# Scaling on ScalarE and a single VectorE rounding in layer 2's quantized attention, and another order of routing for the first batch of its product-key layer

## The chip, the cores and the metric

The kernel runs on one core of a Trainium2 chip. A core has five engines that work side by side, each through its own queue of instructions in order: TensorE (PE in the profile; PEld is its weight load), VectorE (DVE), ScalarE (ACT), GpSimd (POOL) and SyncE (SP). They meet at semaphores, and DMA queues move data beside them. The metric is the device time of one execution in microseconds (us), lower is better. The kernel before has a median of 2180.47 us over three runs (2170.9 to 2184.78).

## The reference

A decoder of four layers, L0 to L3, over 8 sequences of 256 tokens with 256 features (2048 tokens). Each layer has attention, cross attention to a context and a feed-forward part, and after each of the twelve the input is added and the sum is normalised (`_layernorm`). Two neighbours matter here. Layer 2's cross attention is made of linear layers with quantized activations and ternary weights:

```python
def bitnet_linear(x, W, b):
    w_scale = jnp.maximum(jnp.mean(jnp.abs(W)), 1e-05)
    qW = jnp.sign(W) * (jnp.abs(W) > 0.5 * w_scale).astype(W.dtype)
    i_scale = jnp.maximum(jnp.max(jnp.abs(x)), 1e-08) / 127.0
    qx = jnp.clip(jnp.round(x / i_scale), -128.0, 127.0)
    return jnp.einsum('...i,oi->...o', qx, qW) * (w_scale * i_scale) + b
...
vis = bitnet_linear(dinov2_features, W_d2v, b_d2v)
image_embeds = bitnet_linear(vis, W_img, b_img)
fused = bitnet_linear(text_embeddings, W_txt, b_txt)
for Wa, ba in ((W_att0, b_att0), (W_att1, b_att1)):
    kv = bitnet_linear(image_embeds, Wa, ba)
    k = jnp.concatenate([kv, kv], axis=-1)
    attn = softmax(einsum('bse,bpe->bsp', fused, k) * inv_sqrt_e)
    fused = fused + 0.1 * einsum('bsp,bpe->bse', attn, k)
concatenated = [fused, broadcast mean of image_embeds]
h = jax.nn.relu(bitnet_linear(concatenated, W_f1, b_f1))    # 1024 wide
return bitnet_linear(h, W_f2, b_f2)
```

The step `i_scale` is taken from the largest absolute value of a whole activation, so a linear layer can begin only when the whole of its input is known.

Layer 2's feed-forward part looks up experts by product keys and adds a gated MLP:

```python
q = (hidden_states @ Wq.T), two halves of 4 heads
sim = jnp.einsum('pbthn,hkpn->pbthk', q, keys)         # 128 keys each half
sx, ix = top_k(sim[0], 8);  sy, iy = top_k(sim[1], 8)
all_scores = sx[..., :, None] + sy[..., None, :]       # 64 pairs
scores, pk = top_k(all_scores, 8)                      # 8 of 4096 experts a head
w = silu(einsum('btd,bthkd->bthk', x, down_embed[indices])) * softmax(scores)
experts_states = einsum('bthk,bthkd->btd', w, up_embed[indices])
mlp = silu(x @ Wg.T) * (x @ Wu.T) @ Wd.T
return mlp + experts_states
```

## The kernel before

The tokens lie in `self.X` as 16 tiles of 128 tokens (token on the partition) and, transposed, in `self.xT` (feature on the partition, 2 chunks of 128 x 2048). The source is written as generators, `woven` together (each is given with a number of steps and a share, and its steps are spread evenly over that share of the whole); within a stretch a scheduler then orders the instructions of each engine, so that the order on an engine is neither that of the source nor that of another engine. Tiles come from pools with a number of buffers each (`bufs`); an instruction that writes a tile waits until a buffer is free.

**The quantized attention** (`l2_xattn`, L2342). `quantize` (L2232) rounds one chunk with two VectorE instructions: L2236 multiplies by 1/step and adds ROUND, a constant that pushes the fraction out of float32; L2237 subtracts ROUND, takes the minimum with 127 and writes bfloat16. It is used in these places:

- the chunks of context and images, long before (in `prepare_l2_xattn`);
- X: `quantized` and `quantized_steps` (L2279) find the largest value (`all_max`), the step, its reciprocal `x_inv` (`step_of`), and round 8 chunks of 128x512 of `self.xT`; `bit_linear_T` then makes `fused` with TensorE and one VectorE instruction for each of its 8 chunks (L2337);
- the concatenation: after the two attention rounds (`bit_attend`), 8 chunks of `fused`, then the 16 columns of the average `avg` (into `qa`), from which 8 small matmuls and VectorE instructions (L2385) make `bias`, the part of the first linear layer that is the same for every token of a sequence, with its own bias;
- the hidden layer, which is computed twice. The first time (`hidden`, L2398) only the largest value of every row is taken: 4 blocks of 512 tokens x 8 rows of 128 hidden units, one VectorE reduction of 128x512 each into `top`. From it the step of the hidden layer follows. The second time each `hidden` goes through ScalarE as two Relu activations of 128x256 (L2416, scale `s1`, one bias column for a sequence) into `h`, is rounded into `qh` and multiplied by the second weight, eight matmuls into `po` for each of the block's four tiles; VectorE scales `po` and adds the residual (`z`, L2433; GpSimd has made the sum of X and the bias before, L2426), and `finish` normalises two tiles at a time: statistics (L178, L179) and the result X (L202) on VectorE, the reciprocal root on GpSimd (L156, L158), the transposition into xT on TensorE (L188) and ScalarE (L189).

**The product-key layer** (`l2_ffn`, `expert_batches`). It goes by batches of 256 tokens, two tiles each. `route` is a generator: the queries `qT` (L1824), then for each of the two tiles `product_keys` (L1617 on), which takes the 8 best of 128 for each head and half (L1629 copies the similarities on ScalarE; L1632 and L1633 search on VectorE), the 8 best of 64 pairs (L1646, L1647), the row numbers and the softmax (L1660 to L1678), and `compact_picks`, which packs the picks into 14 slots a token and lends the 15th to a token with too many (L1696 to L1746; L1723 writes `index`, L1735 is ScalarE's copy of what TensorE fetched for the lent slots, L1742 reads it). `gated` computes the eight chunks of the gate and up projections and their product `hT` (L1316 Silu on ScalarE, L1317 the product on VectorE).

The picks of a tile are fetched in four groups (4, 4, 4 and 3 rows a token) by GpSimd (`rows`, L1078, an indirect DMA for each of 15 picks) into four row buffers `rows0` to `rows3`, one for each group, used again by the next tile. VectorE takes the dot products with the token (`junk`, L1841), ScalarE their Silu, and TensorE adds the weighted second halves of the rows into `po` by diagonal matrices (L1923; the last row of a group of four goes through VectorE, L1914). `po` also takes the MLP (L1893), and at the end of a tile VectorE adds `rest` (L1931).

Routing of batch b+1 is woven into the picks of batch b (`later`, with the attention of layer 3 and its convolution). Only batch 0 has nothing ahead of it: its own routing, of both tiles, is woven with the gate (`own` beside `gate`) and is finished before its first pick is fetched in the source order.

Of the kernel before, what the change touches and what calls it, by code (L numbers as in the profile page):

```python
# [11 lines left out]
F32 = mybir.dt.float32  # L12
BF16 = mybir.dt.bfloat16
# [3 lines left out]
ALU = mybir.AluOpType  # L17
# [29 lines left out]
class Net:  # L47
# [1741 lines left out]
    def expert_batches(self, w, room, pool, work, ps, general):  # L1789
# [53 lines left out]
        def batch(b, conv, att):  # L1843
# [5 lines left out]
            here, state["routed"] = state["routed"], []  # L1849
            after = route(o + CH, state["routed"]) if b + 1 < B else iter(())  # L1850
# [21 lines left out]
            if b == 0:  # L1872
                for _ in woven((gate, 8, 1.0), (own, 20, 1.0)):
                    pass
            later = woven((gate, 8, 0.42), (after, 20, 0.8), (att, 17, 1.0), (conv, 12, 1.0))
            z = work.tile([P, 2, D], F32, name="z", bufs=1)
            for j in range(2):
                i = 2 * b + j
                x = self.X[:, i, :]
                index, prob, last, slot = here[j]  # L1880
# [357 lines left out]

    def ternary(self, pool):
# [39 lines left out]
    def quantized_steps(self, q, src, name, into, work, *weights, largest=None, bank=None):  # L2279
        n = src.shape[2]  # L2280
        m = self.all_max(src.rearrange("p c n -> p (c n)") if largest is None else largest, into, name, bank)
        inv, scales = self.step_of(m, [q[x][1] for x in weights], into, name)
        dst = into.tile([P, 2, n], BF16, name="q_act")
        for o in range(0, n, 512):
            for c in range(2):
                e = min(o + 512, n)
                self.quantize(dst[:, c, o:e], src[:, c, o:e], inv, work)
                yield
        return dst, scales
# [52 lines left out]
    def l2_xattn(self, w):  # L2342
        nc, tc = self.nc, self.tc
        FC = 8
        with (
# [7 lines left out]
            if True:  # L2353
                with tc.tile_pool(name="x2a", bufs=3, space=PSUM) as ps:
                    qx, (s,) = self.quantized(q, self.xT, "x", pool, work, "txt", largest=self.x_max)
                    self.bit_linear_T(fused, q["txt"][0], qx, s, self.col("l2x_b_txt"), ps)
                with tc.tile_pool(name="x2b", bufs=2, space=PSUM) as ps:
                    for n in range(2):
                        for b in range(B):
                            self.bit_attend(  # L2360
                                fused, kvT[:, n, b * SC : (b + 1) * SC], self.l2x_kv[:, n * B + b, :], b, work, ps
                            )
                            if n:
                                nc.vector.tensor_reduce(
                                    largest[:, b : b + 1], fused[:, :, b * S : (b + 1) * S], AX.XY, ALU.max,
                                    apply_absolute_value=True,
                                )
            m = self.all_max(largest, pool, "cat")
            inv, (s1,) = self.step_of(m, [q["f1"][1]], pool, "cat")
            qf = pool.tile([P, 2, NTOK], BF16, name="q_act")  # L2370
            for o in range(0, NTOK, 512):
                for c in range(2):
                    self.quantize(qf[:, c, o : o + 512], fused[:, c, o : o + 512], inv, work)
            qa = pool.tile([P, 2, B], BF16, name="qa")
            self.quantize(qa.rearrange("p c b -> p (c b)"), avg.rearrange("p c b -> p (c b)"), inv, work)
            w1, (w2, w2_scale) = q["f1"][0], q["f2"]
            with (
# [26 lines left out]
                inv, (s2,) = self.step_of(m, [w2_scale], pool, "hid")  # L2404
                b2 = late.tile([P, D], F32, name="b2")
# [3 lines left out]
                for o in range(0, NTOK, 512):  # L2409
                    qh = work.tile([P, FC, 512], BF16, name="qh")  # L2410
                    for f in range(FC):
                        pp = hidden(f, o)
                        h = work.tile([P, 512], F32, name="h")
                        for b in range(2):
# [6 lines left out]
                                scale=s1,  # L2421
                            )
                        self.quantize(qh[:, f, :], h, inv, work)
# [276 lines left out]
```

## Time and profile before

| what | value |
|---|---|
| median of three runs | 2180.47 us (2170.9 to 2184.78) |
| the profiled execution | 2177.3 us, its span 2175.4 us |
| mean granted TensorE clock | 0.933 of full speed |
| rounding of X, from its step to the end of `fused` | 1254.57 to 1266.59 us |
| the two attention rounds | 1266.65 to 1307 us |
| rounding of the concatenation, until the last row maximum | 1308.06 to 1337.29 us |
| hidden layer, second time | 1338.8 to about 1399 us |
| product-key layer, batch 0: from `qT` to the point where the orders of both kernels meet | 1403.25 to 1533.1 us |

A span is the time from the first to the last recorded instruction. The page gives, for the whole span, the busy time of each engine and the chain of work that ended last; other views give the busy time within a stretch, all instructions of a line or tile with their durations, and the instructions of an engine in order of time. In a timeline a row is: start, duration (of all instructions of the row together), engine, line, operation, output and inputs with shapes, how many, and in brackets how long the engine stood idle before it and what ended that. An average over the whole span says little about one stage: what a change there is worth is read from that stage's rows. Durations come from one execution.

### The profile page before, as it was taken

The numbers are of one execution on the slowest core, as the hardware profiler recorded it, in microseconds if no ns is written. First come the engines' busy times: TensorE is split into PE (matmuls) and PEld (weight loads), VectorE is DVE, ScalarE is ACT, GpSimd is POOL, SyncE is SP. The second block draws the span as 40 slices with busy tenths as digits, with TensorE's granted clock in tenths as the row PEclk, the third lists the DMA queues.
The fourth block names the chain that finished last, engine by engine and source line by source line (L and its number), as shares of the span: only waits on it lengthen the run. The fifth ranks groups of instructions, "written<-read, shape, count | busy, mean of one in ns | idle before, by whom it ended". The sixth has DMA issues, their size and how long they took to land. (4 is left out here: it accounts for less than half of the span.)

```text
span 2175.4 us, 37678 instructions
## 1 busy us (share of the span) xinstructions
PE 1890.9 (87%) x13612; PEld 1399.8 (64%) x13612; DVE 1566.4 (72%) x5213; ACT 891.1 (41%) x1982; POOL 680.8 (31%) x740
## 2 busy tenths in 40 slices
PE   7988699999998988997888877768899999998886
PEld 5765488755556666775555553456777777776775
DVE  5776445356666877765677678789999999976575
ACT  1332343333343334222434332434455554656663
POOL 1012245311111111644443101246444444431232
PEclk9999699999998988998999988888999999999998
DMA  4000355300002101884110010223323233220000
GB/s 138 2 2 13 121 182 172 125 2 1 1 2 92 43 29 46 245 242 121 40 40 21 8 66 10 77 79 93 85 78 86 65 86 90 79 90 15 6 15 21
DMA packets 71684, 148.49 MB, mean 68 GB/s; under 512 B 17000, under 2 KB 40056, under 8 KB 68416
## 3 DMA queue, kind: packets, MB, share of 16 engines
q0 software_dynamic: 32640, 79.46, 12.7%
q1 hardware_dynamic: 34218, 59.35, 8.3%
q10 hardware_dynamic: 4630, 7.16, 0.9%
q8 instruction: 111, 1.82, 0.3%
q14 instruction: 85, 0.70, 0.1%
HBM read 170.35 MB, written 23.24 MB: 89 GB/s over the span
## 5 line engine op out<-in xcount | busy, mean ns | idle before, releaser
L1078 POOL DMA_INDIRECT rows<-in_l2f_table_dram,index x240 | 252.8, 1053 | 280.5 <-PE po L1923 60.4
L146 PE MATMUL pp<-xT,w 128*128 128x256 f32 (+1 forms) x672 | 177.3, 406 | 11.7 <-ACT sim L1629 4.1
L668 POOL TENSOR_TENSOR aT<-sides,inv 128x256 f32<-128x256 f32 x64 | 47.1, 739 | 382.1 <-DVE sides L666 295.1
L146 PEld LDWEIGHTS pp<-xT,w 128*128 128x128 f32 x672 | 127.7, 197 | 37.3 <-ACT qT L1824 5.4
L189 ACT COPY xT<-pt 128x512 f32<-128x512 f32 x88 | 51.3, 585 | 184.1 <-PE pt L188 184.0
L188 PE MATMUL pt<-ident,X 128*128 128x128 f32 x352 | 70.1, 312 | 60.2 <-DVE X L202 44.0
L632 ACT ACTIVATE e<-sc 128x512 f32<-128x512 f32 (+1 forms) x145 | 77.5, 604 | 106.0 <-PE sc L560 82.1
L1923 PE MATMUL po<-rows,diag 128*128 128x256 f32 x384 | 108.7, 403 | 12.7 <-ACT diag L1922 12.2
L560 PE MATMUL sc<-kv,qv 32*128 32x128 f32 (+2 forms) x1540 | 111.5, 335 | 8.7 <-DVE sides L666 3.4
L560 PE MATMUL sc<-qv,kv 32*128 32x128 f32 (+2 forms) x1348 | 109.1, 353 | 3.2 <-DVE qv L614 1.7
L560 PEld LDWEIGHTS sc<-kv,qv 32*128 32x128 f32 x1540 | 88.4, 208 | 35.7 <-issue 20.7
L1078 POOL DMA_INDIRECT xe<-xd,take x83 | 82.4, 992 | 78.4 <-PE pt L1096 33.9
L156 POOL TENSOR_SCALAR rs_v<-ln_mv 128x2 f32<-128x2 f32 (+1 forms) x67 | 19.0, 284 | 279.6 <-DVE ln_mv L179 230.1
L188 PEld LDWEIGHTS pt<-ident,X 128*128 128x128 f32 x352 | 45.1, 154 | 91.3 <-DVE X L202 37.0
L146 PE MATMUL sc<-xT,w 128*128 128x512 f32 (+1 forms) x224 | 100.0, 594 | 2.2 <-DMA w<-in_l0a_wq_dram 1.5
L202 DVE TENSOR_SCALAR X<-z,ln_mv,rs_y 128x256 f32<-128x256 f32 x144 | 55.2, 425 | 59.2 <-POOL rs_y L158 59.1
L1236 ACT ACTIVATE hT<-ph,we_in 128x128 f32<-128x128 f32 x152 | 55.7, 367 | 95.1 <-PE ph L146 90.2
L1841 DVE SCALAR_TENSOR_TENSOR junk<-rows,X 128x256 f32<-128x256 f32 x224 | 93.5, 418 | 1.2
L560 PEld LDWEIGHTS sc<-qv,kv 32*128 32x128 f32 (+1 forms) x1348 | 75.1, 196 | 28.8 <-issue 17.1
L146 PE MATMUL ph<-xeT,we_in 128*128 128x128 f32 x608 | 87.7, 288 | 3.9 <-DMA we_in<-in_l0f_in_dram,wrow 2.5
L146 PEld LDWEIGHTS ph<-xeT,we_in 128*128 128x128 f32 x608 | 76.9, 194 | 15.8 <-ACT hT L1236 11.9
L1923 PEld LDWEIGHTS po<-rows,diag 128*128 128x128 f32 x384 | 68.1, 194 | 28.4 <-ACT diag L1922 16.9
(608 smaller groups left out, 5163.8 us busy)
## 6 DMA issues: line engine op xcount, KB each, us to landing
we<-in_l1f_experts_dram SPq DMA_DIRECT2D x32, 384.0 KB, 4.3
yd<-y SPq DMA_DIRECT2D x32, 256.0 KB
w<-in_l2x_w_dram SPq DMA_DIRECT2D x1, 4096.0 KB
v<-v SPq DMA_DIRECT2D x16, 243.8 KB, 2.7
rows<-in_l2f_table_dram,index POOLq DMA_INDIRECT x240, 3.3
xd<-X SPq DMA_DIRECT2D x8, 257.0 KB, 2.5
xT<-in_xT_dram SPq DMA_DIRECT2D x4, 512.0 KB, 9.2
X<-in_x_dram ACTq DMA_DIRECT2D x8, 256.0 KB
```

The source lines that it names most:

```text
L146: done = self.nc.tensor.matmul(out, lhsT=lhsT, rhs=rhs, start=n == 0, stop=n == last and bias is None)
L156: nc.gpsimd.tensor_scalar(v, var, LN_EPS, None, ALU.add)
L188: nc.tensor.transpose(pt[:, c, j, :], self.X[:, i0 + j * step, c * P : (c + 1) * P], self.ident)
L189: nc.scalar.copy(self.xT4[:, :, i0 : i0 + step + 1 : step, :], pt)
L202: nc.vector.tensor_scalar(self.X[:, i, :], z[:, j, :], mv[:, j, 0:1], r[:, j : j + 1], ALU.subtract, ALU.mult)
L560: nc.tensor.matmul(sc[: shape[0], part], lhsT=lhsT, rhs=rhs, start=mask is None, stop=True, skip_group_check=True)
L632: lambda r, sc: nc.scalar.activation(e0[m][:n0, r], sc, AF.Exp),
L668: nc.gpsimd.tensor_tensor(out, split(both), split(inv), ALU.mult)
L1078: return self.nc.gpsimd.indirect_dma_start(out=out, out_offset=None, in_=table, in_offset=bass.IndirectOffsetOnAxis(ap=index, axis=0), **( ...
L1236: nc.scalar.activation(hT[:, g + f, :], ph[:, f, :], AF.Gelu, bias=b1[:, g + f : g + f + 1])
L1841: nc.vector.scalar_tensor_tensor(junk, row, 1.0, x, ALU.mult, ALU.mult, accum_out=out)
L1923: nc.tensor.matmul(po, lhsT=diag, rhs=rows[:, k, D:], start=j == 0 and (g, k) == (0, 0), stop=j == 1 and (g, k) == (groups[-1][0], here_k ...
```

## The change

In the quantized attention, three of the uses of `quantize` are replaced. For X and for the concatenation ScalarE multiplies a chunk by 1/step (Copy with a scale column, three buffers), and VectorE rounds with one instruction, `rounded`, which adds and subtracts ROUND. In the hidden layer Relu's scale and bias are multiplied by 1/step beforehand (two small VectorE instructions), so that `h` is in steps already and VectorE only rounds it; `h` has three buffers in place of two. The minimum with 127 is dropped. The average's 16 columns are rounded ahead of the 8 chunks of `fused`. In the product-key layer batch 0's routing is woven with the gate only until the first tile's picks exist (`first_tile`); the rest of it, the second tile, stands in front of the other work in `later`, so that it is advanced between the first tile's picks, and what is left of it is finished before the second tile.

In the order of instructions that the build gives, the rest is the same: GpSimd issues the gathers in the same order, and from the second group of batch 1's first tile on all engines have the order of before.

```diff
--- before.py
+++ after.py
@@ -1847,6 +1847,12 @@
                 state["routed"] = []
                 own = route(0, state["routed"])
             here, state["routed"] = state["routed"], []
+
+            def first_tile():
+                while not here:
+                    next(own)
+                    yield
+
             after = route(o + CH, state["routed"]) if b + 1 < B else iter(())
             hT = work.tile([P, FC, CH], F32, name="hT", bufs=1)
 
@@ -1870,13 +1876,16 @@
 
             gate = gated()
             if b == 0:
-                for _ in woven((gate, 8, 1.0), (own, 20, 1.0)):
+                for _ in woven((gate, 8, 1.0), (first_tile(), 10, 1.0)):
                     pass
-            later = woven((gate, 8, 0.42), (after, 20, 0.8), (att, 17, 1.0), (conv, 12, 1.0))
+            later = chain(own, woven((gate, 8, 0.42), (after, 20, 0.8), (att, 17, 1.0), (conv, 12, 1.0)))
             z = work.tile([P, 2, D], F32, name="z", bufs=1)
             for j in range(2):
                 i = 2 * b + j
                 x = self.X[:, i, :]
+                if j == 1:
+                    for _ in own:
+                        pass
                 index, prob, last, slot = here[j]
                 at_end = work.tile([P, 1], F32, name="at_end")
                 dot(at_end, final[:, :D], x)
@@ -2236,6 +2245,14 @@
         nc.vector.tensor_scalar(t, src, inv, ROUND, ALU.mult, ALU.add)
         nc.vector.tensor_scalar(dst, t, ROUND, 127.0, ALU.subtract, ALU.min)
 
+    def rounded(self, dst, src):
+        self.nc.vector.tensor_scalar(dst, src, ROUND, ROUND, ALU.add, ALU.subtract)
+
+    def quantize_scaled(self, dst, src, inv, work):
+        t = work.tile([P, src.shape[-1]], F32, name="quant", bufs=3)
+        self.nc.scalar.activation(t, src, AF.Copy, scale=inv)
+        self.rounded(dst, t)
+
     def ternary(self, pool):
 
         nc = self.nc
@@ -2276,7 +2293,7 @@
             except StopIteration as stop:
                 return stop.value
 
-    def quantized_steps(self, q, src, name, into, work, *weights, largest=None, bank=None):
+    def quantized_steps(self, q, src, name, into, work, *weights, largest=None, bank=None, scaled=False):
         n = src.shape[2]
         m = self.all_max(src.rearrange("p c n -> p (c n)") if largest is None else largest, into, name, bank)
         inv, scales = self.step_of(m, [q[x][1] for x in weights], into, name)
@@ -2284,7 +2301,7 @@
         for o in range(0, n, 512):
             for c in range(2):
                 e = min(o + 512, n)
-                self.quantize(dst[:, c, o:e], src[:, c, o:e], inv, work)
+                (self.quantize_scaled if scaled else self.quantize)(dst[:, c, o:e], src[:, c, o:e], inv, work)
                 yield
         return dst, scales
 
@@ -2352,7 +2369,7 @@
             nc.vector.tensor_reduce(largest[:, B:], avg, AX.XY, ALU.max, apply_absolute_value=True)
             if True:
                 with tc.tile_pool(name="x2a", bufs=3, space=PSUM) as ps:
-                    qx, (s,) = self.quantized(q, self.xT, "x", pool, work, "txt", largest=self.x_max)
+                    qx, (s,) = self.quantized(q, self.xT, "x", pool, work, "txt", largest=self.x_max, scaled=True)
                     self.bit_linear_T(fused, q["txt"][0], qx, s, self.col("l2x_b_txt"), ps)
                 with tc.tile_pool(name="x2b", bufs=2, space=PSUM) as ps:
                     for n in range(2):
@@ -2367,12 +2384,14 @@
                                 )
             m = self.all_max(largest, pool, "cat")
             inv, (s1,) = self.step_of(m, [q["f1"][1]], pool, "cat")
+            qa = pool.tile([P, 2, B], BF16, name="qa")
+            qa_t = pool.tile([P, 2 * B], F32, name="qa_t")
+            nc.vector.tensor_scalar(qa_t, avg.rearrange("p c b -> p (c b)"), inv, None, ALU.mult)
+            self.rounded(qa.rearrange("p c b -> p (c b)"), qa_t)
             qf = pool.tile([P, 2, NTOK], BF16, name="q_act")
             for o in range(0, NTOK, 512):
                 for c in range(2):
-                    self.quantize(qf[:, c, o : o + 512], fused[:, c, o : o + 512], inv, work)
-            qa = pool.tile([P, 2, B], BF16, name="qa")
-            self.quantize(qa.rearrange("p c b -> p (c b)"), avg.rearrange("p c b -> p (c b)"), inv, work)
+                    self.quantize_scaled(qf[:, c, o : o + 512], fused[:, c, o : o + 512], inv, work)
             w1, (w2, w2_scale) = q["f1"][0], q["f2"]
             with (
                 tc.tile_pool(name="x2c", bufs=3, space=PSUM) as ps,
@@ -2402,6 +2421,9 @@
                 nc.vector.tensor_scalar(top, top, 0.0, None, ALU.max)
                 m = self.all_max(top.rearrange("p f b -> p (f b)"), pool, "hid")
                 inv, (s2,) = self.step_of(m, [w2_scale], pool, "hid")
+                in_steps = late.tile([P, 1], F32, name="in_steps")
+                nc.vector.tensor_tensor(in_steps, s1, inv, ALU.mult)
+                nc.vector.tensor_scalar(bias, bias, inv, None, ALU.mult)
                 b2 = late.tile([P, D], F32, name="b2")
                 pp = ps.tile([P, 512], F32, name="pp")
                 nc.tensor.matmul(pp[:, :D], lhsT=self.ones, rhs=b2_row, start=True, stop=True)
@@ -2410,7 +2432,7 @@
                     qh = work.tile([P, FC, 512], BF16, name="qh")
                     for f in range(FC):
                         pp = hidden(f, o)
-                        h = work.tile([P, 512], F32, name="h")
+                        h = work.tile([P, 512], F32, name="h", bufs=3)
                         for b in range(2):
                             n = o // S + b
                             nc.scalar.activation(
@@ -2418,9 +2440,9 @@
                                 pp[:, b * S : (b + 1) * S],
                                 AF.Relu,
                                 bias=bias[:, f, n : n + 1],
-                                scale=s1,
+                                scale=in_steps,
                             )
-                        self.quantize(qh[:, f, :], h, inv, work)
+                        self.rounded(qh[:, f, :], h)
                     for i in range(o // P, o // P + 4, 2):
                         z = work.tile([P, 2, D], F32, name="z")
                         nc.gpsimd.tensor_tensor(
```

## The prediction

> **What bounds the kernel now.** I read the page first (busy shares, then the chain of waits), then the busy time of each engine in the stretches that the diff touches, then the rows of the tiles and the timelines there. Busy shares, and the chain's shares by engine:
>
> ```profile
> PE 1890.9 (87%) x13612; PEld 1399.8 (64%) x13612; DVE 1566.4 (72%) x5213; ACT 891.1 (41%) x1982; POOL 680.8 (31%) x740
> PE 15%; DVE 12%; ACT 2%; POOL 1%; issue 1%; DMA 0%; POOLq 0%; ACTq 0%
> ```
>
> TensorE is the busiest over the span, but the averages hide the edited stages. Busy time by stretch (start:end, length, then each engine's busy us with instructions; then granted TensorE clock, DMA share, GB/s):
>
> ```profile
> 1254.00:1260.00 6.00, 3.05 (x8) 1.19 (x9) 5.59 (x18) 0.00 (x0) 0.00 (x0) 0.60 0.89 373
> 1307.00:1314.00 7.00, 0.58 (x2) 0.50 (x2) 6.29 (x20) 0.00 (x0) 0.00 (x0) 0.50 0.00 0
> 1338.00:1394.00 56.00, 42.17 (x214) 23.27 (x213) 47.76 (x122) 33.37 (x69) 15.14 (x20) 0.85 0.08 29
> 1403.20:1533.10 129.90, 98.94 (x443) 78.90 (x442) 110.73 (x550) 52.68 (x126) 64.09 (x61) 0.87 0.31 87
> 1520.00:1600.00 80.00, 71.51 (x364) 59.62 (x363) 76.23 (x365) 39.64 (x102) 39.18 (x38) 0.96 0.30 81
> ```
>
> The two rounding stretches (first two lines) are VectorE alone: ScalarE stands still and TensorE waits for rounded chunks. The hidden pass (1338 to 1394) has VectorE busy 47.76 of 56, the routing (1403.2 to 1533.1) 110.73 of 129.90, so 19.17 idle; after it VectorE is 95% busy. What is won on VectorE in these places is therefore won for the kernel, as nothing later has slack to absorb it.
>
> **X rounding.** The rows of the tile give 0.478 us for `quant<-xT` and 0.42 for `q_act<-quant`; the timeline has two of the first in 0.88 and two of the second in 0.75, so 0.73 a chunk, 8 chunks from 1254.76 to 1260.62, and then the 8 `fused` (L2337, 5.97 us) end at 1266.6. After: ScalarE scales 128x512 with a scale column. It did not do this form here; nearest is `qv<-turned,consts` (L1026), 0.714 us and two in 1.33, so a pitch of 0.62. The other bounds are the plain 128x512 copy of 0.585 (L189), pitch about 0.5, and `kv` of L1026 at 0.807. Eight copies from 1254.65 end at 1259.7 (7 × 0.62 + 0.71). The build puts VectorE's order as three rounds, one `fused`, two rounds, one `fused`, three rounds, six `fused`. The third round ends at 1257.05, `fused` 1 at 1257.8, rounds 4 and 5 at 1258.6, `fused` 2 at 1259.35, rounds 6 to 8 at 1260.5, six `fused` × 0.746 at 1265.0 to 1265.2. Gain **1.4** (0.4 at 0.8 a copy; 2.3 at 0.5).
>
> The Trainium skill ("ScalarE: Activation LUTs", Rules for kernel authors) says that a multiplication belongs on VectorE and not ScalarE, which speaks against this edit. The rows agree on speed (0.62 against 0.44 a chunk) but not on the advice, since ScalarE shows 0.00 busy here. By that rule alone the gain would be below zero by 8 × 0.18 = 1.4; by the rows it is 1.4.
>
> **Concatenation rounding.** Before: eight chunks from 1308.18 to 1314.1, the average's two operations, eight bias operations (1.64 us) from 1314.79, first row maximum (`top`, L2398) at 1317.14, the 32nd done at 1337.29. After: the average's 16 columns go first, so the bias work (TensorE and VectorE) lies under ScalarE's copies, which run from 1308.15 to 1313.2 by the same pitch. The build's order has seven rounds ahead of the first `top`; the seventh copy ends at 1312.6 and its round at 1313.0, so `top` starts near 1313.1 and one round (0.4) lies among the maxima. The 32 at the old pace (20.15) end at 1333.6. Gain **3.7** (bounds 2.5 and 4.5: copies at 0.8, or at 0.5).
>
> **Hidden pass.** What the rounding costs now, name and count first, then min/median/max ns:
>
> ```profile
> L2236 DVE TENSOR_SCALAR quant<-h,hid_inv x32: 446/485/1315, 1340.6 to 1391.4; 128x512 f32<-128x512 f32 x32
> L2237 DVE TENSOR_SCALAR qh<-quant x32: 411/427/967, 1341.4 to 1391.9; 128x512 bf16<-128x512 f32 x32
> ```
>
> One period (block 2 to block 3) on VectorE, then ScalarE's part in it:
>
> ```profile
> 1363.62 0.87 DVE L2433 SCALAR_TENSOR_TENSOR z<-po,hid_sc,z 128x256 f32<-128x256 f32 x2 [0.31 <-PE po L146]
> ...
> 1370.54 0.73 DVE L202 TENSOR_SCALAR X<-z,ln_mv,rs_y 128x256 f32<-128x256 f32 x2 [0.90 <-POOL rs_y L158]
> ...
> 1371.53 1.71 DVE L2236 TENSOR_SCALAR quant<-h,hid_inv 128x512 f32<-128x512 f32 x2
> ...
> 1378.21 0.87 DVE L2433 SCALAR_TENSOR_TENSOR z<-po,hid_sc,z 128x256 f32<-128x256 f32 x2
> ```
>
> ```profile
> 1372.25 0.59 ACT L189 COPY xT<-pt 128x512 f32<-128x512 f32 x1 [1.55 <-PE pt L188]
> 1372.88 6.57 ACT L2416 ACTIVATE h<-pp,bias,cat_sc 128x256 f32<-128x256 f32 x14
> ```
>
> Four blocks; z to z was 15.29 in the first and 14.8 in the mean (1348.33 to 1392.74, three periods). The layer norms from first z to last X take 7.67 in either kernel. Then seven rounding pairs of 0.91 each run to the next z. The change takes out 32 × 0.485 = 15.5 us of VectorE work, but not all is won. (1) First block: before, ScalarE had two tiles of relu ready by 1339.35, ahead of the step; now relu needs `in_steps` and `bias`·inv, two small operations (0.14 and about 0.3) after 1340.5, and 16 relus at 6.57/14 = 0.47 end at 1348.7, the last round at 1349.15 instead of 1347.75: loss 1.4. (2) Later blocks: three `h` buffers let three tiles be made under the norms; the second xT copy ends 9.25 after z (1372.84 − 1363.62); the build's order leaves three tiles for ScalarE behind that copy, 3 × 0.95, then one round 0.4 and the last po with the joint 0.7: period 13.2. Three periods: 3 × (14.8 − 13.2) = 4.8 gain. Net **3.4**; bounds −0.5 (period 14.5: a fourth tile behind the copy) and 7 (period 12.0: VectorE's 12.6 a block less 3.9 is 8.7, with its two waits for rs_y 10.4; TensorE's 42.17/56 of 14.8 is 11.1, and 0.9 stays for the joint).
>
> In the 1.71 row two operations of 0.44 pitch took 0.83 too long beside GpSimd's `z` add (L2426, 1.20 us). The Trainium skill ("SBUF — State Buffer", Who interferes with whom) calls the port pair of VectorE and GpSimd a lock that one of them holds for its whole instruction, and the trace agrees: 0.83 lost there, 0.54 in a round of 0.97. By the rule every block keeps both collisions, and the sum would change by less than 0.3 a block.
>
> **Routing of batch 0.** VectorE's waits, and the first gather of tile 1:
>
> ```profile
> 1408.19 0.42 DVE L1317 TENSOR_TENSOR hT<-silu,pp 128x256 f32<-128x256 f32 x1 [4.32 <-ACT silu L1316]
> ...
> 1430.20 0.42 DVE L1317 TENSOR_TENSOR hT<-silu,pp 128x256 f32<-128x256 f32 x1 [3.95 <-ACT silu L1316]
> ...
> 1447.80 0.42 DVE L1317 TENSOR_TENSOR hT<-silu,pp 128x256 f32<-128x256 f32 x1 [1.88 <-ACT silu L1316]
> ```
>
> ```profile
> 1454.97 0.99 POOL L1078 DMA_INDIRECT rows<-in_l2f_table_dram,index  x1 [11.64 <-DVE junk L1841]
> ```
>
> No instruction is added; they move. All eight gate products (`hT`) now lie in tile 0's routing, before and just after its index; GpSimd's gathers keep their order; VectorE does the four dots of the first row group ahead of tile 1's searches, the other groups after tile 1's index. Waits that stay: 4.32 and 1.46 at the start, 0.31 of the 0.73 (a product fills the rest), about 1.4 at L1742 (1.35 before), 1.1 for the first rows to land (issue to landing 3.3 median, 7.0 at most; the dots come about 4.8 after the index, the first row is there at about 4.2, the fourth at 8.1), 0.25 and 0.5 small: 9.3. Waits that go: 3.95, 0.61, 0.85, 1.88 and the 1.39 for po (L1893) in the late joint. Idle 19.17 less 9.3 is 9.9, less 1.7 of small gaps (the rows that name a releaser sum to 17.5) 8.2; I take **8.0** (bounds 5 if first rows land at 7.0, 9.5 if the gaps close too). Tile 0's index comes about 1.3 later (three products of 0.42), so its gathers too; tile 1's index stays at about 1444.7 but its first gather starts at about 1445.5 instead of 1454.97, as the first buffer was read long ago. VectorE, 95% busy behind it, is next in line, and the two orders are the same from 1533 on.
>
> **Sum**: 1.4 + 3.7 + 3.4 + 8.0 = 16.5. The profiled execution took 2177.3 (span 2175.4 and 1.9 around it), so 2160.8; the median of the three runs, 2180.47, stands 3.2 above it: **2164**. Under 2158.7 or over 2202.3 is beyond 1%, about what can be told from no change here, as the three runs before spread over 13.9.
>
> **Rivals.**
> *More*: hidden period 12.0, copies at 0.5, routing 9.5: 2.3 + 4.5 + 7 + 9.5 = 23.3, so 2157. For it: ScalarE's queue is empty in the two rounding stretches. Against: its relu and xT copies share a queue in the hidden pass, 8 + 1.2 of 13.2.
> *Routing gives nothing*: VectorE stands before the first rows' dots with tile 1's searches queued behind, and pays in landing what it saved in silu waits: 8.5 remain, 2172. For it: landings to 7.0. Against: the median, 3.3, is within the 4.8 of work ahead.
> *Slower*: the gate products that now precede tile 0's index wait on VectorE's queue for silu as the one at 1430.20 did (3.95: eight matmuls in 3.62 at a low clock, and a 1.28 table load between exp and silu). Five of them at 3.95 are 19.8, less the waits removed (3.95 + 0.61 + 1.88 = 6.4), so 13.4 lost against 8.5 won: 4.9 slower, 2185. It decides from 3.0 a product (14.9 over five). For it: granted clock 0.79 between 1414 and 1423. Against: TensorE idles 5.6 and 2.4 us there, room for four products at 2.0.
> *Not what it says*: rounding a value to another step would change picks, and a tile with too many picks runs the general path; or the order is not as built. About 2180 without a gain.
>
> **How the numbers follow.** Forecast 0.56 (own range 2157 to 2169), more 0.16, routing nothing 0.14, slower 0.10, not as said 0.04. Range 2153 to 2178: from 2157 to 2172, the first three cases, with 4 and 6 beyond for a median of three runs that spread over 13.9 and for the bounds; "slower", "not as said" and the tails, some 0.2, stay out. Faster by over 1%: 0.15 of "more" and 0.08 of the forecast's low end, 0.23. Slower by over 1%: 0.04 of "slower" (waits of 7.4 a product), 0.03 of the last (the general path computes the layer again), 0.07. Within 1%: 0.70.
>
> **What would show it.** Eight ScalarE copies at about 0.62 from 1254.7; the first `top` near 1313 and the last done near 1333.5; z to z of 13.2 in the hidden pass; VectorE idle near 11 us between the qT copy and the first rows of batch 1, and tile 1's first gather about 42 us after that qT copy instead of 51.7. I am wrong if `hT` rows ahead of tile 0's index show waits over 3 us, or if a wait as long as 8 stands before the first dots.

## The result

Over 16 runs each the changed kernel has a median of 2164.08 us (2156.07 to 2173.69), the kernel before 2175.45 (2168.59 to 2185.27): ratio (its time over that of the kernel before) 0.9948, 95% interval 0.9933 to 0.9962, so 11 us faster (8 to 15). The profiled execution took 2163.1 us with a span of 2161.3.

Busy shares and the chain's shares by engine, on the page of the changed kernel:

```profile
PE 1885.8 (87%) x13602; PEld 1398.5 (65%) x13612; DVE 1545.1 (71%) x5167; ACT 901.2 (42%) x1998; POOL 683.1 (32%) x740
PE 15%; DVE 13%; ACT 3%; POOL 2%; issue 1%; DMA 0%; POOLq 0%; ACTq 0%
```

VectorE has 21 us less to do and ScalarE 10 more; the chain is the same mixture. Busy time by stretch (start:end, length, PE, PEld, DVE, ACT and POOL with instructions, granted clock, DMA share, GB/s), for the two rounding stretches, the hidden pass and the routing:

```profile
1248.00:1254.00 6.00, 3.87 (x10) 1.43 (x11) 4.22 (x12) 5.12 (x8) 0.00 (x0) 0.56 0.88 367
1301.20:1308.20 7.00, 4.02 (x23) 2.28 (x25) 5.94 (x24) 5.01 (x8) 0.00 (x0) 0.50 0.01 2
1331.00:1384.00 53.00, 40.22 (x209) 23.14 (x211) 30.84 (x93) 33.34 (x70) 15.20 (x18) 0.84 0.09 30
1392.40:1517.50 125.10, 101.11 (x446) 80.41 (x445) 110.13 (x548) 53.01 (x125) 64.47 (x61) 0.87 0.33 90
```

In the rounding stretches ScalarE now works beside VectorE (5.12 and 5.01 where it had 0.00). In the hidden pass VectorE fell from 47.76 busy of 56 to 30.84 of 53: 17 us less work. The lengths of these two windows are rounded; between the same rows the pass is only 1.4 shorter (the table below: 3.6 won less 2.2 lost). The routing stretch is 4.8 shorter by these windows and 4.5 between the same two rows, with nearly the same VectorE work: 14.97 idle instead of 19.17. In the second pair of executions it is 2.7 shorter.

The first row is ScalarE's new copy, the second what VectorE has left of the hidden pass's rounding:

```profile
L2253 ACT ACTIVATE quant<-xT,x_inv x8: 705/707/721, 1248.7 to 1253.2; 128x512 f32<-128x512 f32 x8
```

```profile
L2249 DVE TENSOR_SCALAR qh<-h x32: 385/426/967, 1333.0 to 1381.1; 128x512 bf16<-128x512 f32 x32
```

Two executions of each program give the stages with their spread (the second ones are experiments 5 and 6); each is measured between the same rows in both kernels (a stage starts with the start of a row, and where its name says "end" or "last row maximum" the end of that row is meant), the last from the first `qT` copy on VectorE (L1824) to the fourth.

| stage, us | before | changed | won, of means | forecast |
|---|---|---|---|---|
| program start to `x_inv` (no edit) | 1254.57, 1248.68 | 1248.45, 1253.63 | | 0 |
| `x_inv` to the end of `fused` | 12.03, 12.05 | 10.51, 10.51 | 1.5 | 1.4 |
| attention rounds, to `cat_inv` (no edit) | 41.39, 44.89 | 43.27, 42.21 | | 0 |
| `cat_inv` to the last row maximum | 29.31, 29.14 | 25.15, 24.77 | 4.3 | 3.7 |
| last row maximum to `hid_inv` | 3.05, 3.05 | 3.96, 4.16 | -1.0 | 0 |
| `hid_inv` to the first `z` | 7.99, 8.00 | 10.54, 9.91 | -2.2 | -1.4 |
| first `z` to the fourth block's (three periods) | 44.42, 44.22 | 40.04, 41.46 | 3.6 | 4.8 |
| `qT` to the fourth `qT` (batches 0 to 2) | 150.29, 149.97 | 146.85, 148.24 | 2.6 | 8.0 |

The forecast's 8.0 for the routing ends earlier, where the orders of both kernels meet; up to that row 3.6 of means is won (129.84 and 129.47 before, 125.39 and 126.77 changed), and 1.0 of it is lost again in the 20 us behind it.

The edited stages win 8.8 in sum, where the forecast had 16.5, and this lies in the interval of the median's 8 to 15. In this table stages with identical instructions differ by up to 6 us between executions, so two profiled spans (2175.4 and 2161.3) cannot be subtracted to judge an edit. The gains of X and of the concatenation are far beyond the spread of their own stages (0.4 at most). That of the routing is not: with the experiments' profiles (those of 4, 7, 8 and 11, which have other orders, and 12 left aside) the new order takes 146.2 to 148.9 and the old one 150.0 to 153.3. So the new order is faster in every one of them, but by how much, 1 to 7, these profiles don't settle.

### The profile page after: what moved, and what is told of

It reads as the page before. It is cut to its first block, busy times and chain, and to the rows that moved or that the text cites. A ratio compares the mean times of both kernels' runs of the same rounds, so it can differ in the third digit from the quotient of the medians.

```text
span 2161.3 us, 37633 instructions
## 1 busy us (share of the span) xinstructions
PE 1885.8 (87%) x13602; PEld 1398.5 (65%) x13612; DVE 1545.1 (71%) x5167; ACT 901.2 (42%) x1998; POOL 683.1 (32%) x740
## 5 line engine op out<-in xcount | busy, mean ns | idle before, releaser
L560 PEld LDWEIGHTS sc<-qv,kv 32*128 32x128 f32 (+1 forms) x1348 | 74.0, 195 | 28.7 <-issue 17.1
```

What stands on the lines that cost most here:

```text
L560: nc.tensor.matmul(sc[: shape[0], part], lhsT=lhsT, rhs=rhs, start=mask is None, stop=True, skip_group_check=True)
```

## The experiments

**1 and 2. Each half alone.** The attention edit with the old routing, and the new routing with the old attention:

```diff
-                for _ in woven((gate, 8, 1.0), (first_tile(), 10, 1.0)):
+                for _ in woven((gate, 8, 1.0), (own, 20, 1.0)):
...
-            later = chain(own, woven((gate, 8, 0.42), (after, 20, 0.8), (att, 17, 1.0), (conv, 12, 1.0)))
+            later = woven((gate, 8, 0.42), (after, 20, 0.8), (att, 17, 1.0), (conv, 12, 1.0))
```

(experiment 1; experiment 2 is the kernel before with these hunks the other way round)

> Only the quantized attention is changed; routing as before. Theory (gains are local and add up; the hidden pass gives most of its gain back in its first block): X to the end of fused 10.5 to 11.0 us from its reciprocal (before 12.0), concatenation to the last row maximum 25.2 (before 29.3), first block of the hidden pass 10.5 from its reciprocal to its first z (before 8.0), z to z 13.3 (before 14.8); sum 6 to 7, ratio 0.9970. Rival 1 (the median's gain of 11 is all from these VectorE instructions, routing gives nothing): ratio 0.995. Rival 2 (what VectorE does less becomes waits, and the gain is all routing): ratio 1.000.

> Only the routing of batch 0 is changed; the quantized attention as before. Theory: VectorE's idle time from the first qT copy to the point where the orders meet is 15 (before 19.2), that stretch 125 (before 129.9), ratio 0.998. What I forecast (idle 11, stretch 122): ratio 0.9963. Rival (a longer half-clock stretch behind it gives it back): ratio 1.000.

Attention alone: ratio 0.9985 (0.9967 to 1.0003). Its stages came as the theory says: X 10.51, concatenation 24.65, first block 9.56, three periods 41.59. The whole time did not follow: by these stages some 6 us are won, by the medians 4. In the profiled execution two stages that this kernel doesn't edit were long, the attention rounds (45.17) and the first three batches (153.3 with the old routing, granted clock 0.84, where the kernel before has 150.0 to 150.3 at 0.86). Routing alone: 0.9988 (0.9970 to 1.0006); VectorE stands idle 19.7 from the first `qT` to the fourth instead of 20.6 to 20.9, and that stretch is 148.9 long, 1.0 to 1.4 shorter than before and not the 8 shorter that ratio 0.9963 needs. Up to the row where the orders meet it is 127.6 with 17.1 idle, where the theory had 125 and 15.

The profiled execution of experiment 2 (2177.6) lies 4.7 above its median, and shows where such time can go. Behind the fourth `qT` copy VectorE has the same order in both kernels, and there the late batches ran at another clock. One of them from `qT` to `qT`, in the kernel before and in experiment 2:

```profile
1692.11:1762.00 69.89, 67.07 (x368) 54.82 (x367) 66.61 (x335) 39.19 (x97) 31.89 (x30) 1.00 0.29 78
```

```profile
1688.03:1759.60 71.57, 68.75 (x367) 56.03 (x366) 66.83 (x335) 39.19 (x96) 31.84 (x30) 0.98 0.28 77
```

From the fourth `qT` to the end of the program the profiles of experiments 2, 8 and 11 have 626.3 to 626.5, the others with this order 621.9 to 622.5 (experiment 12 aside). Whether the other executions of these three kernels are like that is not known.

Each half's interval holds 1, so neither is shown to be faster by its whole time. Rival 1 of the first expectation (0.995) lies outside the interval of the attention alone and falls; that the gain is all routing (rival 2) would need about 0.995 of the routing alone and falls by its interval. Both halves together multiply to 0.9973, a little short of 0.9948, but the intervals leave room for it.

**3. The first tiles of the hidden pass ahead of the step.**

```diff
+                        ahead = o == 0 and f < 3
...
-                                scale=in_steps,
+                                scale=s1 if ahead else in_steps,
...
-                        self.rounded(qh[:, f, :], h)
+                        if ahead:
+                            self.quantize(qh[:, f, :], h, inv, work, bufs=3)
+                        else:
+                            self.rounded(qh[:, f, :], h)
```

(the scaled bias has a tile of its own, so that the first three tiles can read the other)

> The changed kernel, but the first three tiles of the hidden pass's first block keep the old relu and the two-instruction rounding, so that ScalarE can make them before the step is known. Theory (the first block lost 2.6 because ScalarE stood still until in_steps and TensorE then ran at half clock): from the reciprocal to the first z 6.5 to 7.5 instead of 10.5, z to z unchanged at 13.3, ratio to before 0.993 (0.9948 less 3 to 4 us). Rival (the first block is bound by its eight tiles on TensorE at the low clock, whoever waits): 9.5 to 10.5, ratio 0.9945.

Ratio 0.9956 (0.9939 to 0.9972), the first block 8.86: between the theory's 6.5 to 7.5 and the rival's 9.5 to 10.5. VectorE's last row before the first `z` shows why. Its timeline (start, us, engine, line, operation, output and inputs, count, idle before and what ended it):

```profile
1335.87 0.43 DVE L2249 TENSOR_SCALAR qh<-h 128x512 bf16<-128x512 f32 x1 [0.73 <-ACT h L2440]
1338.76 0.88 DVE L2460 SCALAR_TENSOR_TENSOR z<-po,hid_sc,z 128x256 f32<-128x256 f32 x2 [2.47 <-PE po L146]
```

VectorE finishes rounding 6.4 us after the reciprocal and then waits 2.47 for TensorE. The same first block, by stretch (the first number after the length is TensorE's busy time, the last but two the granted clock), in the kernel before, then the changed one, then this one:

```profile
1340.50:1348.50 8.00, 6.76 (x39) 3.68 (x39) 7.53 (x20) 7.31 (x17) 0.00 (x0) 1.00 0.00 0
```

```profile
1331.50:1342.00 10.50, 8.91 (x40) 4.93 (x41) 3.90 (x13) 9.12 (x20) 0.00 (x0) 0.67 0.00 0
```

```profile
1330.00:1339.00 9.00, 8.14 (x37) 4.61 (x36) 4.83 (x16) 5.96 (x13) 0.00 (x0) 0.62 0.00 0
```

The matmuls are about the same (39, 40, 37), but take 6.76 us at clock 1.00 and 8.91 or 8.14 at 0.67 and 0.62. Both causes are there: ScalarE's late start, which the edit mends for three tiles, and TensorE's low clock, which it doesn't. What sets the clock is not shown: with the changed kernel's instructions in this block experiment 1 had 0.82 and took 9.56.

**4. Four gate products in tile 0's routing instead of eight.**

```diff
-                for _ in woven((gate, 8, 1.0), (first_tile(), 10, 1.0)):
+                for _ in woven((islice(gate, 4), 4, 1.0), (first_tile(), 10, 1.0)):
...
-            later = chain(own, woven((gate, 8, 0.42), (after, 20, 0.8), (att, 17, 1.0), (conv, 12, 1.0)))
+            later = chain(woven((gate, 4, 1.0), (own, 10, 1.0)), woven((gate, 8, 0.42), (after, 20, 0.8), (att, 17, 1.0), (conv, 12, 1.0)))
```

> The changed kernel, but only four of the eight gate products are woven into the first tile's routing; the other four stand with the second tile's routing. The order of later batches is different as well, so that only the stretch up to the second tile's index is compared. Theory (the waits of 1.64 and 1.48 at the sixth and seventh product are what kept the gain at 4.7 instead of 8): these two waits go, the first index comes 19 to 20 after the qT copy (changed kernel 21.0, before 19.7), and VectorE idles 10 to 11 instead of 13. Rival (TensorE's half clock there moves the same waits to the next products): idle stays at 13.

Ratio 1.0126 (1.0096 to 1.0157). Tile 0's index came 19.70 after the `qT` copy, as expected, but tile 1's 24.46 after it instead of 21.6 to 21.9, and no waits were won: the two went, but up to tile 1's index VectorE still waits some 11, as in the changed kernel. The loss is elsewhere: the scheduler put the later batches in another order. One period of the late batches, by stretch, in the changed kernel and in this one:

```profile
1671.40:1741.30 69.90, 67.06 (x366) 54.80 (x366) 66.63 (x332) 39.19 (x97) 31.93 (x31) 1.00 0.28 78
```

```profile
1644.30:1721.40 77.10, 69.76 (x367) 57.36 (x366) 68.66 (x333) 36.53 (x94) 31.51 (x30) 0.93 0.26 69
```

Nearly the same instructions take 6 to 7 us longer in each such batch. For the first stage this is inconclusive, and experiment 8 asks it again with the later order kept.

**5 and 6. Both kernels profiled once more**, without an edit.

> The kernel before, profiled once more, for the spread of the stages between executions of the same program. Theory (what the changed kernel lost outside the edited lines is TensorE's clock, which differs from execution to execution): X 12.0, concatenation 28.9 to 29.3, first block 8.0, three periods 44 to 44.5, but the unchanged attention rounds anywhere from 41 to 45 and the time before the X reciprocal anywhere from 1244 to 1255. Rival (the attention rounds are slower in the changed kernel because of the change): attention rounds 41.4 to within 0.5.

> The changed kernel, profiled once more. Theory: X 10.5, concatenation 24.7 to 25.2, first block 9 to 10.6, three periods 40 to 41.6, first three batches of the product-key layer 146.8 to 149; attention rounds between 41 and 45. Rival (as above): attention rounds 43.3 to 45.2 again.

The table above has the numbers. The attention rounds took 44.89 in the kernel before and 42.21 in the changed one, so the rival falls. The stretch of these rounds in the kernel before, in its two executions, with 195 matmuls in both:

```profile
1266.60:1308.00 41.40, 30.94 (x195) 24.60 (x195) 30.79 (x92) 18.00 (x80) 0.00 (x0) 0.94 0.00 1
```

```profile
1260.73:1305.62 44.89, 34.70 (x195) 27.16 (x195) 31.13 (x92) 17.94 (x80) 0.00 (x0) 0.83 0.00 1
```

VectorE and ScalarE work the same time; TensorE takes 3.8 longer at clock 0.83 than at 0.94, and the stretch is 3.5 longer.

**7. Queries and first similarities ahead of the gate.**

```diff
-                for _ in woven((gate, 8, 1.0), (first_tile(), 10, 1.0)):
+                first = first_tile()
+                next(first)
+                next(first)
+                for _ in woven((gate, 8, 1.0), (first, 8, 1.0)):
```

> The changed kernel, but two steps of the first tile's routing (queries and first similarities) are taken ahead of the first gate product. Theory (VectorE's first wait, 4.9 us, is TensorE making a gate product that nobody needs yet): the first top comes 4.9 after the qT copy instead of 6.9, tile 0's index 19 after it instead of 20.95, the first three batches take 145 to 146.5, ratio 0.994. Rival (TensorE's work only changes its place and is waited for at a later product): index at 20.5 to 21, ratio 0.995.

Ratio 0.9958 (0.9941 to 0.9974). The first `top` came 3.5 after the `qT` copy instead of 6.9, but the index only 0.5 earlier, at 20.49, and the products just before and behind the index wait 1.45, 0.88 and 1.30. The stretch of three batches is 146.4, at the lower edge of the changed kernel's 146.8 to 148.2 (and experiment 9, which leaves the routing as changed, has 146.2). The rival is nearer.

**8. Five gate products woven in, the other three left to the sum of tile 0.** The new line of experiment 4's first pair, with five in place of four, and `later` as in the changed kernel.

> The changed kernel, but five gate products are woven into the first tile's routing, and the last three come when the first tile's sum needs them; the order of batch 1 onward is nearly that of the changed kernel. Theory (my forecast fell short by the products that stand between tile 0's searches and its last picks): tile 0's index 19.7 after the qT copy, VectorE's waits between it and the first rows' dots 1.5 to 2 instead of 3.6, q1 to q3 145 to 146.5. Rival (TensorE is next in line, so the three products are waited for later in tile 0 or 1): index 19.7 but q1 to q3 147 to 149.

Ratio 0.9966 (0.9948 to 0.9984). The index came at 19.86, and then, on VectorE's timeline:

```profile
1413.83 0.42 DVE L1317 TENSOR_TENSOR hT<-silu,pp 128x256 f32<-128x256 f32 x1 [1.92 <-ACT silu L1316]
1416.67 0.43 DVE L1841 SCALAR_TENSOR_TENSOR junk<-rows,X 128x256 f32<-128x256 f32 x1 [0.75 <-DMA rows<-in_l2f_table_dram,index]
1417.97 0.43 DVE L1841 SCALAR_TENSOR_TENSOR junk<-rows,X 128x256 f32<-128x256 f32 x1 [0.47 <-DMA rows<-in_l2f_table_dram,index]
1419.33 0.43 DVE L1841 SCALAR_TENSOR_TENSOR junk<-rows,X 128x256 f32<-128x256 f32 x1 [0.60 <-DMA rows<-in_l2f_table_dram,index]
1436.78 0.69 DVE L1824 COPY qT<-pp 128x512 f32<-128x512 f32 x1 [1.83 <-PE pp L146]
```

One product's wait is gone, and 1.8 us of waiting for the first gathered rows is there instead, behind which batch 1's queries wait 1.83 for TensorE. The stretch is 147.9: the rival holds.

**9 and 12. The hidden edit taken out of the changed kernel, and put alone into the kernel before.** The hunks of the change from `in_steps` to `self.rounded(qh[:, f, :], h)`, undone or done alone (undone with three `quant` buffers).

> The changed kernel with the hidden pass as before (two VectorE instructions a tile, two buffers of h, scale s1); everything else as changed. Theory (the hidden edit nets about 0.5 us: the periods win 3.4, the first block loses 2.0 and the two operations ahead of the step 0.9): from the last row maximum to the qT copy 66 (changed kernel 65 to 66), ratio 0.995. What I forecast (net 3.4): that stretch 69, ratio 0.9965. Rival (VectorE's 15.5 us of multiplications count in full): ratio 1.002.

> The kernel before with the hidden edit alone (scaled relu, one VectorE rounding, three buffers of h); X, concatenation and routing as before. Theory (the hidden edit nets 0.4 to 1.2 us by its stages): from the last row maximum to the qT copy 65 to 66 (before 66 to 66.3), first block 9.5 to 10.5 (before 8.0), three periods 40 to 41.6 (before 44.3), ratio 0.9995 with an interval that holds 1. Rival (the whole-time difference between the changed kernel and the one without this edit, 0.9948 against 0.9976, is the edit's own): ratio 0.997.

Without it: ratio 0.9976 (0.9961 to 0.9992); from the last row maximum to the `qT` copy 66.2 (changed 65.0 and 66.0). Alone: 0.9991 (0.9972 to 1.0009), that stretch 63.1 against 65.8 and 66.0, with a first block of 9.64 and periods of 39.9 together. (In that last comparison both kernels were some 63 us slower than in the others; only its ratio and stages are used.) So by its stages the edit is worth 0.2 to 2.8. That VectorE's 15.5 us of removed multiplications count in full is excluded by both runs: the ratio would be 1.002 in the first and 0.993 in the second. The whole time of experiment 9 says more than its stages: its interval leaves out the theory's 0.995 and holds the 0.9965 of the forecast's 3.4. Why 0.9976 lies so far from 0.9948 is not explained; the two intervals only just overlap. Experiment 12's interval holds the theory's 0.9995 and just leaves out the rival's 0.997, but its stretch of 63.1 is shorter than the theory's 65 to 66.

The two operations ahead of the step are long in experiment 9 too (the stretch from the last row maximum to `hid_inv`, called head from here on, is 3.96), where the hidden pass is the old one, and the head is 3.05 in experiment 12: this loss comes with the concatenation's edit, and is 1.0 of what experiment 12 has won beyond the theory.

**10. The row b2 made earlier.** Its four lines (tile, PSUM tile, matmul, copy) are moved ahead of `top`.

> The changed kernel, but the row b2 is made ahead of the row maxima, so that GpSimd's first two additions of X and b2 are long done when VectorE forms the hidden step. Theory (the two operations of 64 columns take 1.35 and 0.99 because GpSimd adds at the same time): from the last row maximum to the reciprocal 2.0 to 2.3 instead of 3.96, those two operations about 0.28 and 0.13 to 0.28, ratio 0.994. Rival (they wait for something else, such as the end of the maxima): 3.9.

Ratio 0.9940 (0.9922 to 0.9959), head 2.10. The two operations in the changed kernel and what GpSimd does then, and below it the same in this experiment:

```profile
1327.42 1.35 DVE L2420 SCALAR_TENSOR_TENSOR top<-top,cat_sc,bias 128x64 f32<-128x64 f32 x1
1328.80 0.99 DVE L2421 TENSOR_SCALAR top<-top 128x64 f32<-128x64 f32 x1
```

```profile
1327.42 2.31 POOL L2448 TENSOR_TENSOR z<-X,b 128x512 f32<-128x512 f32 x2 [82.43 <-DVE top L2417]
```

```profile
1329.37 0.28 DVE L2424 SCALAR_TENSOR_TENSOR top<-top,cat_sc,bias 128x64 f32<-128x64 f32 x1
1329.68 0.20 DVE L2425 TENSOR_SCALAR top<-top 128x64 f32<-128x64 f32 x1
```

With GpSimd's adds elsewhere the two take 0.28 and 0.20 instead of 1.35 and 0.99: the theory on them is right. (The whole time can't tell: the interval holds 0.9948.) In the kernel before the first one started 0.06 ahead of the add and only the second (1.14) was held up; the earlier finish of the maxima moved the first one into the add as well. The adds now lie in the concatenation stretch, which grew from 25.0 to 25.9, so about 1.0 of the 1.9 is left.

**11. Three corrections in one**: b2 early, the whole first block in the old way (`ahead = o == 0`), and experiment 7's order.

> The changed kernel with three corrections: the bias row early, the whole first block of the hidden pass with the old relu and two-instruction rounding, and queries and first similarities ahead of the first gate product. Theory (each is worth what its stage showed): head 2.0 to 2.3 (changed kernel 3.96), first block 7.5 to 8.2 (9.9 to 10.5), q1 to q3 146.4 (148), so 5 to 6 us off the changed kernel, ratio 0.992 to 0.993. Rival (what is won there is lost again to the clock or at the next wait): ratio 0.995.

Ratio 0.9937 (0.9911 to 0.9962), median 2160.58. Head 2.60, first block 7.21, three batches 146.6, concatenation 25.6: by its stages 4.7 better than the changed kernel. In the first block the granted clock was 1.00, as before the change, and the block is 0.8 shorter than there. The profiled execution lost 4.3 again behind the fourth `qT`, where the late batches took 71.6 instead of 69.9 as in experiment 2. It is the fastest of all, but its interval holds 0.9948, so that it beats the changed kernel is not shown by the whole time.

## Why the prediction was right, and where it wasn't

The time came out on the forecast, 2164, and that it did so to the microsecond is luck. The base was 5 too high: the forecast took 2180.47, the median of three runs, and the longer series has 2175.45. The gain was 5 too high as well: 11 by the medians and 8.8 by the stages, against 16.5. With the base of the longer series the forecast would have been 2159, still inside its range.

**X and concatenation: right, with the sizes.** ScalarE's copy is 0.707 with a pitch of 5.22/8 = 0.65 or 5.01/8 = 0.63 (forecast 0.714 and 0.62); the gains 1.5 and 4.3 (1.4 and 3.7). The row of a like instruction with the same shape, elsewhere in the program, priced the new one's duration within 1%. As to the Trainium skill's rule against multiplying on ScalarE ("ScalarE: Activation LUTs", Rules for kernel authors), which by itself would have made X lose 1.4: the rows disagree (1.5 won), since the slower engine was idle.

**Hidden pass: mechanism right, sizes off.** Three periods won 3.6 (forecast 4.8: 13.3 and 13.8 each in the mean, single ones 12.5 to 14.8, for 13.2). They are set by ScalarE's relu as said: in the changed kernel the last rounds of a block wait for it one by one:

```profile
1352.35 0.43 DVE L2249 TENSOR_SCALAR qh<-h 128x512 bf16<-128x512 f32 x1 [1.85 <-ACT h L2438]
1353.26 0.43 DVE L2249 TENSOR_SCALAR qh<-h 128x512 bf16<-128x512 f32 x1 [0.48 <-ACT h L2438]
1354.17 0.43 DVE L2249 TENSOR_SCALAR qh<-h 128x512 bf16<-128x512 f32 x1 [0.48 <-ACT h L2438]
```

The first block lost 2.2 (1.4): ScalarE's late start was counted, the low clock of this block was not (0.67, where the kernel before has 1.00; TensorE had run 0.65 us of matmuls in the 4.6 us before the block's first one). And the operations ahead of the step lost 1.0, forecast at nothing; the sentence on GpSimd's adds looked at one place of the collision and not at where the shift would move the next. Two small sums of the working don't come out as they stand: 16 relus of 0.47 from 1340.94 end at 1348.5 and not 1348.7, so a loss of 1.15, and a fourth tile behind the copy gives a period of 14.15 and not 14.5.

**Routing: the term that failed.** "Waits that stay ... 9.3" measured 13.3, and 14.6 in the second execution, so that the 8.0 became 3.6. Point by point:

| VectorE's waits, us | forecast | changed | second execution |
|---|---|---|---|
| at the start | 6.1 | 7.25 | 7.24 |
| around L1742 | 1.4 | 3.64 | 2.50 |
| for the first rows | 1.1 | 0 | 0.82 |
| after that | 0.75 | 2.44 | 4.03 |

The products at the sixth and seventh place, just behind the index, waited for TensorE:

```profile
1415.71 0.42 DVE L1317 TENSOR_TENSOR hT<-silu,pp 128x256 f32<-128x256 f32 x1 [1.64 <-ACT silu L1316]
1418.39 0.42 DVE L1317 TENSOR_TENSOR hT<-silu,pp 128x256 f32<-128x256 f32 x1 [1.48 <-ACT silu L1316]
1419.34 0.25 DVE L1742 SCALAR_TENSOR_TENSOR junk<-w,consts 128x32 f32<-128x32 f32 x1 [0.52 <-ACT w L1735]
```

TensorE made two products in 6.53 us there, the clock being 0.50 from 1410.3 to 1417.1; at the 1.99 of a product at full clock it would have been 4. What was removed (3.95, 0.61, 1.88, 1.39) is indeed gone, and tile 0's index came 1.3 later as said, but the second execution shows 1.83 at batch 1's queries and 1.47 at a search, both for TensorE. "VectorE, 95% busy behind it, is next in line" was wrong for this stretch: TensorE is, and in experiment 8 the gathered rows too. Experiments 7 and 8 show it, since each wait taken away came back at a later product, at the first rows or at a query. The rival in which products wait for silu is what happened in kind, behind the index and not ahead of it, with 1.6 at most in the changed kernel and not the 3.0 a product at which it decides. The prediction's sign of being wrong, an `hT` row ahead of the index with a wait over 3, was badly drawn: the first product waited 4.93 (4.45 in the second execution), but the forecast itself kept 4.32 there.

Tile 1's first gather came 46.4 after `qT` (42 forecast, 51.7 before). GpSimd stood idle 4.16 before it, though its index was written 3.35 earlier. In all ten profiles with the new order this distance is 3.34 or 3.35, in experiment 4 too, where VectorE has other instructions behind the index; what held the gather is open. No row shows VectorE waiting for these rows.

## What to carry to other kernels

Take work off the busy engine only together with a look at who sets the pace once it is gone: 17 us less VectorE work in the hidden pass gave 1.4 us, as ScalarE's relu and TensorE at a low clock took over. Scaling ahead of a step that isn't known yet ends the run-ahead, so keep the old form for the first block (7.21 in experiment 11, 10.2 in the changed kernel). Judge an edit by its own stages in several executions, with the unedited stages beside it as a measure of the spread.

## What was not expected

- The same program's unedited stages differ from execution to execution: the attention rounds took 41.1 to 45.2 in thirteen profiles, with a granted clock of 0.95 in the shortest and 0.82 in the longest, and the start of the program to `x_inv` 1243.6 to 1257.0 (the profile of experiment 12 not counted).
- Two VectorE operations of only 64 columns take 0.28 and 0.20 alone, and 1.35 and 0.99 when GpSimd adds 128x512 twice beside them. This bears out "SBUF — State Buffer" (Who interferes with whom) in the Trainium skill, by which whichever of the two engines issues first holds their shared port pair for its whole instruction: here two short operations together took 2.34, about as long as the two adds (2.31).
- A change of four steps in the source's order of batch 0 made the scheduler order the batches behind it otherwise, and the kernel 1.3% slower with nearly the same instructions.
